# A transformer block with routed experts: parts of an expert's list and register loads become steps of the attention's plan

## The chip, the cores and the metric

The kernel runs on one core of a Trainium2 chip. The metric is the device time of one execution in microseconds (us), as the median of several. Engines are named as in the profile: PE multiplies matrices (PEld is its weight load, which overlaps), DVE is the vector engine, ACT the scalar engine, POOL GpSimd, SP SyncE, which only issues DMAs here. Each engine works through its own queue in order.

## The reference, cut to what matters

```python
# B = 2 batches of T = 2048 tokens, D = 256; 2 heads of 128 with one shared K and V; 8 experts, FF = 1024
mod = (silu(c) @ wmod).reshape(B, 6, 1, D)          # sa, ca, ga, sb, cb, gb
h = layernorm(x) * (1 + ca) + sa
k = rope(h @ Wk.T); v = h @ Wv.T; q = rope(einsum('btd,hkd->bhtk', h, Wq))
w = softmax(where(causal, q k^T / sqrt(128), -inf))
x = x + ga * ((w v) @ Wo.T)

h = layernorm(x) * (1 + cb) + sb
gate = softmax(h @ Wg + bg)                          # [4096, 8]
thr = sigmoid(h @ Wt + bt) / 8
w = relu(gate - thr);  w = w / sum(w)                # many entries are zero
u = gelu(einsum('td,edf->etf', h, W1) + b1)
x = x + gb * einsum('te,etd->td', w, einsum('etf,efd->etd', u, W2) + b2)
```

All is float32. A token has to be worked on only by the experts for which its weight is not zero; the kernel makes use of that.

## The kernel before

The program has two phases.

**Attention.** `attention()` handles 32 tiles of 128 tokens (16 of each batch), in groups that alternate between the batches: `(0,4),(1,4)` three times, then `(0,2),(1,2),(0,1),(1,1),(0,1),(1,1)`. It doesn't emit instructions directly. Every piece of work is a step that is given to a plan: `plan.add(engine, cost, do, after, take, give, rank, late)`. `cost` is a written estimate of its time, `late` what passes until its effect is there (a DMA's landing), `take` and `give` count buffers, and a low `rank` goes first. `Plan.run` (L36 to L88) simulates the engines with these costs, takes for a free engine the ready step with the lowest rank, and emits all steps in the order so found. On the chip this order is fixed for each engine.

For a tile the steps are: layer norm, transposition, projections, scores (L528 on PE, then a copy with maximum L539 on DVE and the exponential L555 on ACT), transposed probabilities (L601, L605), the sums with V (pav, L611), projection (L645), residual (L652), second layer norm (L412 to L419, L667, L670), writing of the normalised features to a table in HBM (`feats`), and the gate's logits (L692 and on). For each group, `gate_steps` works out each token's weight for each expert, and the place that it takes in that expert's list (`place`, `entry`). One list for each expert lies in HBM; an entry holds the token's number and weights. List 0 is written during attention: one indirect DMA of POOL for each tile (`scatter`, L808), each after the one before.

Three further things are done in attention, with rank 1000, so behind everything else: the front of list 0 is read (`read_front`, L906), and expert 0's first 512 entries that lie in it are worked on ahead, as two items of 256 tokens (AHEAD = 2). An item is: `fetch` (gather of the tokens' features by POOL, L884; transposition by a DMA of SP, L893; `join` on DVE, L899), `first` (W1, PE, L950), `act` (Gelu, ACT, L958), `second` (W2, PE, L967), `result` (DVE, L974 to L979). Then the whole sheet of list 0 is read (L1005), `behind` (DVE, L1012) takes the numbers of the item that follows, and `fetch` brings its columns to `kept.xT`. `total` (PE and DVE, L852 to L871) sums up how many tokens each expert has, and how many items; the counts lie in `counts`.

**Experts.** `experts()` has a loop for each engine, over experts and items, with semaphores between the engines and with the counts in registers. `count` loads a count into an engine's register (L1038, a TENSOR_LOAD on that engine's queue), at the head of each engine's part or at each expert. An item of expert e takes 256 tokens of its list (the last one may be half as wide):

- POOL copies the numbers from the sheet (L1299) and gathers the features (L1257); SP transposes them (L1103); DVE joins them into xT (L1199).
- PE: h = W1 (L1145), y = W2 (L1136), ACT: Gelu between them (L1171).
- DVE scales with weight and modulation (L1208, L1214, L1223, L1235), POOL adds the rows to the output by an indirect DMA (L1288).

While expert e runs, POOL writes list e+1 with `write`: NP = 8 parts of NW = 4 tiles, one part (four scatters, L1278) for each item of expert e, and in front of the first item those parts for which e has no items. SP reads the sheet of e+1 (L1093) after as many turns of its loop as there are parts in items (`a`), once all parts are written. ACT issues the weight load for expert e+2 when it begins expert e (L1180, L1183).

Part 0 of list 1 is written once before the loop (`write(1, 0, 0)`), so that the semaphore `written` starts one part up, and once more in the loop.

Of the kernel before, what the change touches and what calls it, by code (L numbers as in the profile page):

```python
# [18 lines left out]
ALU = mybir.AluOpType  # L19
AX = mybir.AxisListType  # L20

P = 128
# [10 lines left out]
NW = 4  # L33
NP = NTOK // P // NW
AHEAD = 2
AHEAD_TILES = 24  # L36
SC = 512
# [64 lines left out]
def adaln_block_kernel(ctx, tc, x, wqkvT, woT, wgt, bgt, w1, b1T, w2, b2, cT, wmod, rope, out):  # L102
# [50 lines left out]
        who=const.tile([P, CI], I32, name="who"),  # L153
        xT=const.tile([P, KD, TI], F32, name="xT"),
    )

# [36 lines left out]
def attention(  # L193
# [83 lines left out]
    l_c = load(c_sb, cT.rearrange("(k p) b -> p k b", p=P), 2)  # L277
    l_x0 = None
    wm = wmod.rearrange("(k p) f -> p k f", p=P)
# [144 lines left out]
    def tile_steps(b, i, r, group, g):  # L424
# [225 lines left out]
        def resid():  # L650
            for h in range(NH):
# [3 lines left out]
                )  # L655

        n_a = add("ACT", 0.38, aT_out, n_p[-1:], take=["aT"], give=["pav"])
        n_o = add("PE", 0.87, proj, [n_a, m_wo[b]], take=["ps"], give=["aT"])
# [57 lines left out]
    def gate_steps(b, i0, m, q, group, after):  # L716
# [89 lines left out]

        def scatter(j):
            nc.gpsimd.indirect_dma_start(  # L808
                out=lists[0],
                out_offset=bass.IndirectOffsetOnAxis(ap=place[:, at + j, 0:1], axis=0),  # L810
                in_=entry[:, at + j, 0, :],
                in_offset=None,
            )
# [7 lines left out]
        n = add("DVE", 1.2, places, [n_c, n_w], give=["ps"])  # L821

        for j in range(m):
            listed.append(plan.add(
                "POOL", 1.1, lambda j=j: scatter(j), after=[n] + listed[-1:], rank=r + 10.0,
                late=1.5,
            ))
        return n

    order_w, listed, last_exp = [], [], []  # L830
    groups = [(0, 4), (1, 4)] * 3 + [(0, 2), (1, 2), (0, 1), (1, 1), (0, 1), (1, 1)]
    begun, q = [0] * B, 0
    for b, m in groups:
        group, ends = {}, []
        for j in range(m):
            ends.append(tile_steps(b, begun[b] + j, float(q + j), group, j))
        last = gate_steps(b, begun[b], m, q, group, ends)
        begun[b] += m
        q += m
        if q == AHEAD_TILES:  # L840
            listed_ahead = list(listed)

            def filled(group=group):
                pf = ps_tile("pf")
                nc.tensor.matmul(pf[:, :1], ones, group["sum"][:, :1], start=True, stop=True)
                nc.vector.tensor_scalar(flag, pf[:, :1], float(AHEAD * TI), None, ALU.is_ge)

            n_flag = plan.add("PE", 0.2, filled, after=[last], take=["ps"], give=["ps"], rank=q)

    def total():  # L850
# [14 lines left out]
        )  # L865
        nc.vector.reduce_sum(n, more, axis=AX.X)
        nc.vector.tensor_copy(counts[:, E : 2 * E], n)
        nc.vector.tensor_scalar(
            counts[:, 2 * E : 3 * E], n, -1.0, float(NP), ALU.mult, ALU.add
        )  # L870
# [5 lines left out]

    def fetch(index, u, after, to, take=()):

# [28 lines left out]

    n_front = low("SP", 0.1, read_front, listed_ahead + last_score, late=2.5)

# [12 lines left out]
    for k in range(AHEAD):  # L922
# [61 lines left out]
        for f0 in range(0, NF, 2):  # L984
            n = low(
                "PE", 1.74, lambda f0=f0, first=first: first(f0), [n_x, l_first[0]] + before_gelu,
                take=["ps"], give=["s"] if f0 == NF - 2 else [],
            )
            n_a.append(low(
                "ACT", 1.0, lambda f0=f0, act=act: act(f0), [n, l_b1] + before_gelu + n_a[-1:],  # L990
                take=["s"], give=["ps"],
            ))
        n = None
        for c in range(CI):
            for f0 in (0, NF // 2):
# [5 lines left out]
                )  # L1001
        low("DVE", 1.5, result, [n, n_g, l_b2], give=["ps", "size"])

    n_s = low(
        "SP", 0.1, lambda: nc.sync.dma_start(kept.sheet, sheet_of_0), listed, late=2.0  # L1005
    )
# [11 lines left out]

    n = low("DVE", 0.4, behind, [n_s, n_flag])
    fetch(lambda c: next_at[:, c : c + 1], "_next", [n], lambda: kept.xT)  # L1020

    plan.add("PE", 0.2, total, after=[last, n_flag], take=["ps"], give=["ps"], rank=q)
    plan.run()
    ctx.close()


def experts(
# [6 lines left out]
    LAG = 2  # L1034
    xT, who, yo = kept.xT, kept.who, kept.yo[-1]

    def count(eng, at, most):
        return nc.values_load(  # L1038
            counts[0:1, at : at + 1], engines=[eng.engine],
            skip_runtime_bounds_check_because="from a sum of 0s and 1s over all tokens",  # L1040
            min_val=0, max_val=most,
        )

# [34 lines left out]
    with tc.tile_critical():  # L1078
# [7 lines left out]
        with nc.Block() as block:  # L1086

            @block.sync
            def _(sync):
                def read(e):  # L1090

                    sync.wait_ge(sem["written"], (e * NP + 1) * (16 * NW))
                    sync.dma_start(  # L1093
                        sheets[e], lists[e].rearrange("(p c) f -> p c f", p=P)
                    ).then_inc(sem["read"], 16)
# [11 lines left out]
                for e in range(E):  # L1107
                    many = items_of(sync, count(sync, e, NTOK))
                    if e == E - 1:
                        run(sync, many, NTOK // TI, lambda i: turn(t0 + i))  # L1110
                    else:
                        a = count(sync, E + e, NP)
                        run(sync, a, NP, lambda i: turn(t0 + done + i))
# [13 lines left out]
            def _(pe):  # L1127
# [31 lines left out]
                pe.sem_inc(sem["taken"], 1)  # L1159
                n = [count(pe, e, NTOK) for e in range(E)]  # L1160
                items(pe, n, item, begin)

            @block.scalar
            def _(act):
# [22 lines left out]
                act.sem_inc(sem["second"], 4)  # L1187
                items(act, [count(act, e, NTOK) for e in range(E)], item, begin)

            @block.vector  # L1190
            def _(dve):
# [50 lines left out]

                n = [count(dve, e, NTOK) for e in range(E)]
                skip = count(dve, 3 * E, AHEAD * CI)
                dve.sem_inc(sem["ready"], 2)
# [3 lines left out]
            def _(pool):  # L1249
# [13 lines left out]

                def write(e, c, w=None):

                    if w is None:
                        w = c + (e - 1) * NP
                        wait("written", w * (16 * NW) + 16 * NW)
                        w = w + 1
                    pool.tensor_copy(  # L1270
# [59 lines left out]
                pool.sem_inc(sem["biased"], AHEAD)  # L1330
                write(1, 0, 0)
                skip = count(pool, 3 * E, AHEAD * CI)
                done, t0 = 1, 0
                for e in range(E):
                    many = items_of(pool, count(pool, e, NTOK))
                    if e > 0:
# [3 lines left out]
                    else:  # L1340
                        a, front = count(pool, E + e, NP), count(pool, 2 * E + e, NP)

                        def part(c):
                            write(e + 1, nc.s_assert_within(c, 0, NP - 1,
                                skip_runtime_bounds_check_because="a part of a list"))

                        run(pool, front, NP, part)
                        run(pool, a, NP, lambda i: item(
# [19 lines left out]
                single = pool.snap(  # L1368
                    ((count(pool, E - 1, NTOK) + (P - 1)) >> 7) & 1, min_val=0, max_val=1
                )  # L1370
# [54 lines left out]
```

## Time and profile before

| | |
|---|---|
| median of 3 runs | 1676.8 us (1675.76 to 1677.0) |
| profiled execution | 1677.0 us, span of its instructions 1675.2 us |
| granted TensorE clock, mean | 0.988 |
| PE busy | 1622.3 us, 97% |
| POOL busy | 855.0 us, 51% |
| DVE busy | 677.0 us, 40% |
| ACT busy | 576.4 us, 34% |
| last matmul of the items ahead ends | 499.5 us |
| first matmul of the experts' loops | 506.9 us |

"Busy" is the time in which an engine runs instructions; loads of registers, branches, semaphores and the issue of DMAs don't count as busy. In a line of the table of groups, `L1145 PE MATMUL h<-xT,w ... x2752 | 660.6, 373 | 16.3 <-DVE xT L1199 8.9` means: line 1145 of the kernel, on PE, matmuls that write h from xT and w, 2752 of them, 660.6 us busy, 373 ns on average, and before them PE stood idle for 16.3 us, of which 8.9 us ended with the release by DVE's line 1199. In a line of a timeline the start comes first, then the length, and in brackets the idle time of the engine before it and what ended it. A `q` behind an engine's name is its sequencer (DMA issue, register loads). "PEclk" is the granted clock as a share of full speed.

### The profile page before, as it was taken

How to read it: one execution, taken by the hardware profiler on the slowest of the kernel's cores; microseconds unless marked ns; L12 is line 12 of the kernel's file. 1: busy time of each engine (PE TensorE's matmuls, PEld its weight loads, DVE VectorE, ACT ScalarE, POOL GpSimd, SP SyncE). 2: the span in 40 equal slices, each digit the busy share in tenths (PEclk: the TensorE clock that was granted, in tenths of full speed). 3: DMA queues.
4: the chain of work that ended last, by engine and by line, in shares of the span. 5: the costliest groups of instructions: out<-in, count | busy, mean ns of one | idle time of the engine just before them, and what ended most of it. 6: DMA issues, size and time to landing. Idle time of an engine off the chain costs nothing.

```text
span 1675.2 us, 26699 instructions
## 1 busy us (share of the span) xinstructions
PE 1622.3 (97%) x7666; PEld 1352.3 (81%) x7666; DVE 677.0 (40%) x2220; ACT 576.4 (34%) x1390; POOL 855.0 (51%) x991
## 2 busy tenths in 40 slices
PE   6999999999998998999999999999999999999996
PEld 3667677676787887888888888888888888888886
DVE  5987767666642222322333222222322222222322
ACT  2555555555632222222222222222222232222222
POOL 2332222021117777756775775676677477734443
PEclk9999999999998998999999999999999999999998
DMA  6211000000024334335334433533533333433332
GB/s 218 101 39 32 26 29 29 17 13 17 13 50 101 57 63 109 58 58 108 58 60 101 78 57 61 106 59 62 109 60 61 63 58 57 67 59 57 63 57 47
DMA packets 166045, 106.36 MB, mean 63 GB/s; under 512 B 111136, under 2 KB 157344, under 8 KB 165856
## 3 DMA queue, kind: packets, MB, share of 16 engines
q0 software_dynamic: 42064, 46.84, 17.8%
q1 hardware_dynamic: 116048, 46.22, 11.7%
q10 hardware_dynamic: 7872, 12.58, 2.4%
q8 instruction: 26, 0.43, 0.1%
q14 instruction: 35, 0.29, 0.1%
HBM read 50.39 MB, written 31.87 MB: 49 GB/s over the span
## 4 chain that ended last, share of the span: by engine, by line
PE 61%; DMA 3%; issue 3%; POOL 3%; POOLq 1%; DVE 0%; SPq 0%; DVEq 0%
PE h L1145 31%; PE y L1136 30%; POOL out L1288 2%; DMA xp<-xr 1%; DMA xr<-feats,at 1%; POOL list L1278 0%; POOL xr L1257 0%; DMA out<-yo,who 0%; POOLq L1038 0%; POOL out L1320 0%; POOL at L1299 0%; POOLq L1086 0%; POOLq L1299 0%; DVE yo L1235 0%; POOL to L1270 0%
## 5 line engine op out<-in xcount | busy, mean ns | idle before, releaser
L1145 PE MATMUL h<-xT,w 128*128 128x256 f32 (+1 forms) x2752 | 660.6, 373 | 16.3 <-DVE xT L1199 8.9
L1136 PE MATMUL y<-w,g 128*128 128x256 f32 x2640 | 654.3, 379 | 0.0
L1171 ACT ACTIVATE g<-h,b_sb 128x256 f32<-128x256 f32 (+1 forms) x688 | 320.4, 466 | 847.8 <-PE h L1145 845.7
L1145 PEld LDWEIGHTS h<-xT,w 128*128 128x128 f32 x2752 | 514.7, 191 | 86.6 <-DVE xT L1199 10.5
L1136 PEld LDWEIGHTS y<-w,g 128*128 128x128 f32 x2640 | 498.8, 190 | 66.3
L1288 POOL DMA_INDIRECT out<-yo,who x173 | 283.2, 1637 | 215.1 <-DVE yo L1235 163.0
L1199 DVE COPY xT<-xp 128x512 uint16<-128x512 uint16 x172 | 68.0, 437 | 630.4 <-PE h L1145 608.0
L1278 POOL DMA_INDIRECT list<-new,to x228 | 233.7, 1025 | 99.3 <-POOL new L1273 46.7
L1257 POOL DMA_INDIRECT xr<-feats,at x172 | 173.8, 1010 | 100.9 <-POOL at L1299 70.2
L611 PE MATMUL pav<-pT,v 128*128 128x256 f32 x544 | 144.0, 387 | 0.6 <-ACT pT L605 0.5
L528 PE MATMUL psc<-kT,qT 128*128 128x512 f32 (+3 forms) x320 | 142.9, 532 | 0.3 <-DVE s L539 0.2
L539 DVE TENSOR_SCALAR_CACHE_REDUCE s<-psc 128x512 f32<-128x512 f32 (+3 forms) x160 | 96.2, 605 | 68.3 <-PE psc L528 46.0
L555 ACT ACTIVATE s<-s,nmx 128x512 f32<-128x512 f32 (+3 forms) x160 | 103.9, 651 | 46.5 <-DVE nmx L546 46.2
L611 PEld LDWEIGHTS pav<-pT,v 128*128 128x128 f32 x544 | 96.1, 192 | 29.1 <-issue 19.6
L1223 DVE TENSOR_TENSOR yb<-y,b_bc 128x256 f32<-128x256 f32 x165 | 62.6, 419 | 135.9 <-PE y L1136 135.8
L418 POOL TENSOR_SCALAR rstdf<-mvf 128x1 f32<-128x1 f32 x32 | 8.3, 260 | 195.2 <-DVE mvf L414 115.4
L605 ACT COPY pT<-ptr 128x512 f32<-128x512 f32 (+1 forms) x144 | 77.2, 563 | 52.3 <-PE pav L611 30.4
L601 PE MATMUL ptr<-ident,s 128*128 128x128 f32 x544 | 76.4, 280 | 2.7 <-ACT s L555 2.7
L601 PEld LDWEIGHTS ptr<-ident,s 128*128 128x128 f32 x544 | 65.6, 145 | 16.6 <-ACT s L555 5.0
L1214 DVE SCALAR_TENSOR_TENSOR gate<-gb_bc,mcur,part 128x256 f32<-128x256 f32 x172 | 75.8, 482 | 3.0
L808 POOL DMA_INDIRECT list<-entry,place x32 | 33.7, 1054 | 76.9 <-DVE place L805 56.6
L528 PEld LDWEIGHTS psc<-kT,qT 128*128 128x128 f32 x320 | 57.5, 190 | 14.0 <-issue 6.3
(157 smaller groups left out, 1069.7 us busy)
## 6 DMA issues: line engine op xcount, KB each, us to landing
w<-in_w ACTq DMA_DIRECT2D x12, 1024.0 KB, 7.8
x<-in_x SPq DMA_DIRECT2D x32, 128.0 KB, 2.1
out<-x SPq DMA_DIRECT2D x32, 128.0 KB, 1.7
w<-in_w SPq DMA_DIRECT2D x4, 1024.0 KB, 9.1
feats<-hp SPq DMA_DIRECT2D x32, 128.0 KB, 1.7
list<-new,to POOLq DMA_INDIRECT x228
out<-yo,who POOLq DMA_INDIRECT x173
xr<-feats,at POOLq DMA_INDIRECT x172, 2.8
```

The costliest lines, as they stand in the source:

```text
L528: nc.tensor.matmul(ps[:, :w], st["qT"][:, h, :], kT[:, ds(c * SC, w)], start=True, stop=not last)
L539: nc.vector.tensor_scalar(s[:, :w], st["sc", h, c][:, :w], 1.0, None, ALU.mult, ALU.max, accum_out=st["mx", h][:, c : c + 1],)
L555: nc.scalar.activation(s[:, :w], s[:, :w], AF.Exp, bias=st["nmx", h], accum_out=st["den"][:, h, c : c + 1],)
L601: nc.tensor.transpose(ptr[:, j, h, :], s[:, ds((c0 + j) * P % SC, P)], ident)
L605: nc.scalar.copy(pT[:, :m], st["ptr", c0][:, :m])
L611: nc.tensor.matmul(st["pav"][:, : NH * P], v[:, c0 + j, :], st["pT", c0][:, j].rearrange("p h t -> p (h t)"), start=(c0 + j == 0), stop=(c ...
L1136: last = pe.matmul(ys[c], gs[f % 4][:, ts(c, P)], weights[e][1][:, f, :], start=(f == 0), stop=(f == NF - 1),)
L1145: last = pe.matmul(hs[f % 4][:, :w], weights[e][0][:, k, ts(f, P)], xT[:, k, :w], start=(k == 0), stop=(k == KD - 1),)
L1171: act.activation(gs[f % 4][:, :w], hs[f % 4][:, :w], AF.Gelu_apprx_tanh, bias=b1_sb[:, at : at + 1],).then_inc(sem["act"], 1)
L1257: pool.indirect_dma_start(out=xr[:, ts(c, 2 * D)], out_offset=None, in_=feats, in_offset=bass.IndirectOffsetOnAxis(ap=at[:, c : c + 1], ax ...
L1278: pool.indirect_dma_start(out=lists[e], out_offset=bass.IndirectOffsetOnAxis(ap=to[:, j : j + 1], axis=0), in_=new[:, j, :], in_offset=Non ...
L1288: pool.indirect_dma_start(out=rows, out_offset=bass.IndirectOffsetOnAxis(ap=who[:, c : c + 1], axis=0), in_=yo[:, c, :], in_offset=None, b ...
```

## The change

1. A constant FRONT = 2. The first two parts of list 1 (8 tiles of batch 0) are written by steps of the plan, as those of list 0 are. In the loops, list 1 has six parts left, and the count of parts for expert 0 is at most six. `written` starts at 16, by one scatter that writes the first tile's entries again, and the waits for it are rewritten to match.
2. The loads of the counts into registers become steps of the plan (`hold`), one for each engine, of rank 1000: PE's after `total` and the last matmul ahead, ACT's after the last Gelu ahead, DVE's after `behind`, POOL's after `total`, SP's after the read of the sheet. Counts that aren't held are loaded in the loops as before.
3. `behind` and the next item's `fetch` have rank 999 instead of 1000.
4. `read_front` waits only for the scatters of list 0 that it reads, and no longer for the last tile's scores too. The matmuls of the items ahead wait for the last tile's last sum with V (`last_sum`) instead of the last exponential.
5. `total` is a step with `late=2.0`, and limits the parts for expert 0 (two small DVE operations more).

```diff
+FRONT = 2
+        last_sum[:] = n_p[-1:]
@@ gate_steps
-        def scatter(j):
+        def scatter(e, j):
             nc.gpsimd.indirect_dma_start(
-                out=lists[0],
-                out_offset=bass.IndirectOffsetOnAxis(ap=place[:, at + j, 0:1], axis=0),
-                in_=entry[:, at + j, 0, :],
+                out=lists[e],
+                out_offset=bass.IndirectOffsetOnAxis(ap=place[:, at + j, e : e + 1], axis=0),
+                in_=entry[:, at + j, e, :],
                 in_offset=None,
             )
...
         for j in range(m):
-            listed.append(plan.add(
-                "POOL", 1.1, lambda j=j: scatter(j), after=[n] + listed[-1:], rank=r + 10.0,
-                late=1.5,
-            ))
+            for e in (0, 1):
+                if e == 0 or at + j < FRONT * NW:
+                    listed[e].append(plan.add(
+                        "POOL", 1.1, lambda e=e, j=j: scatter(e, j), after=[n] + listed[e][-1:],
+                        rank=r + 10.0 * (e + 1), late=1.5,
+                    ))
@@ total
         nc.vector.reduce_sum(n, more, axis=AX.X)
+        nc.vector.tensor_scalar(n[:, :1], n[:, :1], float(NP - FRONT), None, ALU.min)
@@ items ahead
-    n_front = low("SP", 0.1, read_front, listed_ahead + last_score, late=2.5)
+    n_front = low("SP", 0.1, read_front, listed_ahead, late=2.5)
...
-                "PE", 1.74, lambda f0=f0, first=first: first(f0), [n_x, l_first[0]] + before_gelu,
+                "PE", 1.74, lambda f0=f0, first=first: first(f0),
+                [n_x, l_first[0]] + last_sum,
...
-    n = low("DVE", 0.4, behind, [n_s, n_flag])
-    fetch(lambda c: next_at[:, c : c + 1], "_next", [n], lambda: kept.xT)
-    plan.add("PE", 0.2, total, after=[last, n_flag], take=["ps"], give=["ps"], rank=q)
+    n_behind = next_("DVE", 0.4, behind, [n_s, n_flag])
+    fetch(lambda c: next_at[:, c : c + 1], "_next", [n_behind], lambda: kept.xT, low=next_)
+    n_total = plan.add(
+        "PE", 0.2, total, after=[last, n_flag], take=["ps"], give=["ps"], rank=q, late=2.0
+    )
+    def hold(name, eng, columns):
+        def load():
+            kept.count[name] = {at: register(nc, eng, counts, at) for at in columns}
+        return load
+    skip = 3 * E
+    low("PE", 2.0, hold("PE", nc.tensor, range(E)), [n_total] + n_ahead)
+    low("ACT", 2.0, hold("ACT", nc.scalar, range(E)), [n_total] + n_a)
+    low("DVE", 2.2, hold("DVE", nc.vector, [*range(E), skip]), [n_total, n_behind])
+    low("POOL", 1.0, hold("POOL", nc.gpsimd, [skip, 0, E, 2 * E]), [n_total])
+    low("SP", 0.5, hold("SP", nc.sync, [0, E]), [n_total, n_s])
@@ experts, SP
-                    sync.wait_ge(sem["written"], (e * NP + 1) * (16 * NW))
+                    sync.wait_ge(sem["written"], (e * NP - FRONT) * (16 * NW) + 16)
@@ experts, all engines
-        return nc.values_load(...)
+        held = kept.count[eng_name[eng.engine]]
+        return held[at] if at in held else register(nc, eng, counts, at)
@@ experts, POOL
-                def write(e, c, w=None):
-                    if w is None:
-                        w = c + (e - 1) * NP
-                        wait("written", w * (16 * NW) + 16 * NW)
-                        w = w + 1
+                def write(e, d):
+                    first = FRONT if e == 1 else 0
+                    w = d + ((e - 1) * NP - FRONT if e > 1 else 0)
+                    c = nc.s_assert_within(d + first, first, NP - 1, ...)
+                    wait("written", w * (16 * NW) + 16)
...
-                write(1, 0, 0)
+                pool.indirect_dma_start(
+                    out=lists[1],
+                    out_offset=bass.IndirectOffsetOnAxis(ap=place[:, 0, 1:2], axis=0),
+                    in_=entry[:, 0, 1, :],
+                    in_offset=None,
+                ).then_inc(sem["written"], 16)
```

## The prediction

> **What bounds the kernel now.** I read the page first, for the engine that is busy, then its table of costly groups, for the idle time in front of that engine's groups, and then windows and timelines around that idle time.
>
> ```profile
> PE 1622.3 (97%) x7666; PEld 1352.3 (81%) x7666; DVE 677.0 (40%) x2220; ACT 576.4 (34%) x1390; POOL 855.0 (51%) x991
> L1145 PE MATMUL h<-xT,w 128*128 128x256 f32 (+1 forms) x2752 | 660.6, 373 | 16.3 <-DVE xT L1199 8.9
> ```
>
> PE is the bound, at 97%. The change adds and removes no matmul, so it can only act on PE's idle time (1675.2 - 1622.3 = 52.9 us of the span) and on what idle time costs afterwards through the clock. In the second phase the whole idle time in front of the first matmul of an item is 16.3 us, and nearly all of it lies in two places. The windows cut there show both:
>
> ```profile
> core 0: us, PE busy (x) PEld busy (x) DVE busy (x) ACT busy (x) POOL busy (x), PEclk, DMA share, GB/s
> 462.00:500.00 38.00, 37.46 (x184) 32.45 (x183) 15.99 (x76) 14.74 (x30) 7.67 (x9) 1.00 0.21 51
> 500.00:507.00 7.00, 0.14 (x1) 0.15 (x1) 1.69 (x5) 0.00 (x0) 3.36 (x4) 0.63 0.24 29
> 507.00:523.30 16.30, 16.30 (x64) 13.93 (x65) 2.47 (x7) 3.79 (x8) 11.39 (x16) 0.84 0.57 167
> 523.30:627.20 103.90, 103.90 (x497) 91.56 (x496) 31.98 (x86) 29.50 (x64) 76.27 (x86) 1.00 0.36 60
> 627.20:636.20 9.00, 0.06 (x2) 0.04 (x1) 0.85 (x3) 0.00 (x0) 6.08 (x6) 0.74 1.00 286
> 636.20:652.70 16.50, 16.50 (x64) 14.08 (x65) 3.45 (x11) 3.79 (x8) 12.22 (x15) 0.83 0.33 55
> 652.70:1662.00 1009.30, 1009.30 (x4769) 890.26 (x4768) 298.34 (x835) 283.35 (x608) 627.66 (x651) 1.00 0.39 68
> ```
>
> The first place is the step from attention to the experts' loops (500 to 507), the second is expert 0's last item (627.2 to 636.2). From 652.7 to 1662 PE has no gap at all. The clock column matters: the item after each gap runs at 0.83 to 0.84, and its 64 matmul rows take 16.3 and 16.5 us, where an item at clock 1.00 takes 13.85 (103.90 us for seven and a half). So a gap costs its own length and about 2.7 us more.
>
> Why the second gap is there, from the timeline:
>
> ```profile
> 617.56 0.35 SPq L1093 DMA_DIRECT2D sheet<-list  x1
> 625.97 0.38 ACTq L1180 DMA_DIRECT2D w<-in_w  x1
> 626.54 1.58 SPq L1103 DMA_TRANSPOSE xp<-xr  x1
> 635.35 0.76 DVE L1199 COPY xT<-xp 128x512 uint16<-128x512 uint16 x2 [9.83 <-DMA xp<-xr]
> 636.17 1.22 PE L1145 MATMUL h<-xT,w 128*128 128x256 f32 x2 [8.94 <-DVE xT L1199]
> ```
>
> SyncE reads expert 1's sheet after eight turns, because list 1 is written in eight parts, one for each item of expert 0, which has nine items here. The gather for expert 1's first item then starts at 621.84, its transposition is issued at 626.54, behind the 1 MB weight load of 625.97, and ends 8.5 us after it. DMA share is 1.00 in that window. Usually this transposition takes 3.1 us.
>
> Why the first gap is there, from the waits and the register loads of the counts:
>
> ```profile
> PEld h L1145 <- DVEq L1038: 7.8, 1, 7.8
> PE h L1145 <- DVEq L1038: 7.4, 1, 7.4
> L1038 DVEq TENSOR_LOAD <-counts x9: 299/310/570, 503.1 to 506.3; - x9
> L1038 PEldq TENSOR_LOAD <-counts x8: 294/306/622, 502.8 to 505.5; - x8
> ```
>
> The last matmul of the items ahead ends at 499.46. DVE copies xT until 501.73, all engines meet, and then DVE loads nine counts (503.1 to 506.6) before it says that xT is ready; PE's first matmul follows at 506.86.
>
> **The change, part by part.**
>
> *Two parts of list 1 are written during attention.* L1278 falls from 228 to 217: 36 scatters for list 1 before (a part was written twice), now 6 x 4 and one that only moves the count. The sheet of expert 1 is now due after six parts: two turns earlier, two items of 13.8 = 27 us. Its gather can then go when xr is free, in place of behind the sheet. The trace holds this very case: at expert 1 to 2, where the sheet is long there, the gather is issued 6.3 us before the half item, the transposition at 775.76, before the weight load at 783.11, and PE goes on at 784.20 with no gap. Two turns of slack are many times what is needed. So the 8.94 us go, and the clock stays: 8.94 + 2.7 = **-11.7 us**. What is late next is nothing on PE: ScalarE's weight load follows the transposition, as at 783.
>
> *Eight more scatters in the plan (L808, 32 to 40).* Eight times 1.074 us (the median of L808) on POOL, which is about a quarter busy in attention. Each waits for the one before in the same list, 2.2 us to landing, where the plan writes 1.1 + 1.5; queued behind such a wait on POOL stand the small moments of the next tile (L418, L419), on which DVE's normalisation waits. L808 already waited for itself 14 times for 17.5 us, with no PE gap to show for it: PE's gaps from 71 to 455 add up to only some 4 us. Bounds: 0 (all beside PE) and 8 x 1.07 = 8.6 us x a tenth reaching PE. I take +0.3. Here a rule speaks against the change. L808 takes 1.074 us in attention, with DVE two thirds busy, and L1278 0.977 in the experts' loops, with DVE a third busy: 0.1 us apiece, 0.8 us in all, under POOL's idle time. The Trainium skill, "SBUF — State Buffer", section "A bandwidth-pool intuition that's wrong (but worth ruling out)", says that VectorE can lock GpSimd out of the shared port, and that a DMA whose descriptors GpSimd writes then took some 3100 ns in place of 620. By that factor of five, eight scatters would cost 8 x 1.07 x 4 = 34 us of POOL; with a tenth of it on PE the sum below would be -10. The trace has 32 of these scatters among the same work, the longest at 1.271; I go by it.
>
> *Front of the sheet of list 0 read earlier.* The read (SP), the gathers (POOL, 2 x 1.2), the weights and gates (DVE, seven operations, 2.6 us in all by their rows) and the joins move from the last tile of the batch pair two tiles up, since the read no longer waits for the last scores. SP queues it in front of a tile's `out`, and DVE's part may wait for the landing, with scores' maxima behind it that ScalarE's exponentials wait for. The plan counts 2.5 us of landing and the trace has 1.5; but the scatters it waits for land 0.7 us a link later than planned. I put DVE's wait at 1.8 us, of which half reaches PE: +0.9. In return, the 2.12 us gap at 454.95 (ScalarE's exponentials late, beside the present read at 452.63) may shrink, and its cold time of 1.7 us too; of the 3.8 I take a tenth off: -0.4. DVE's two more tiny operations in the counting step: +0.15. Attention together: 0.3 + 0.9 - 0.4 + 0.15 = **+1.0 us**, bounds -2 (most of the gap of 455 gone) and +4 (a new gap like it, with its cold clock).
>
> *The matmuls of the items ahead wait for the last tile's last sum, not its exponential.* In the order of the instructions PE's queue near its end stays all but the same: the first of them follows the last pav, as before. I cost this at 0; what hides it is PE itself, which is full there (37.46 of 38.00).
>
> *The counts as steps of the plan, the next item's columns in front.* DVE's nine loads now stand between next_at and the first result, where DVE is 42% busy (15.99 of 38): 3.5 us off the path, at 0. ACT's eight stand behind its last Gelu, POOL's and SP's early: 0. PE's eight, though, stand at the very end of PE's queue, behind its last matmul: 499.46 + 3.0 (their time in the trace) = 502.5, where DVE is ready at 501.73. Everyone then meets 0.8 us later than now. From there, before: DVE came out 1.37 us after its xT, and PE started 0.26 us after DVE's last load. So PE starts at 502.5 + 1.37 + 0.26 = 504.1; PE's own entry to its loop, at most 1.06 us after its last load, gives the same. 506.86 - 504.1 = **-2.7 us**. Bounds: -1 (loads are slower while DMA runs: single ones took 622 ns) and -3.5. PE idles some 4.6 us still. Does the clock go cold? In this trace the gap of 2.12 us at 455 was followed by a clock of 0.5 from 457.5, that of 7.40 went cold 2.2 us in, that of 8.94 only 4.3 us in. The Trainium skill, "TensorE: Matmul & The Clock Gate", "What's actually happening", has half clock after about one idle window of 3.4 us that runs free of the program. By the rule 4.6 us is a matter of luck and the sum may be -16.0 (2.6 us more); by the rows it is -13.4, as two of three gaps were cold sooner. I leave the cold item in.
>
> Weights of expert 2 are now issued some 2 us earlier (505.14 before), and the first gather's transposition comes later than the landing of 7.8 us: 0.
>
> **Sum**, against the profiled execution (span 1675.2, time 1677.0, so 1.8 us lie around the span; it is 0.2 above the median of 1676.8): -11.7 - 2.7 + 1.0 = -13.4. Span 1661.8; from the median, **1663.4 us**.
>
> **The rivals.**
>
> A, *the second gap does not close entirely*. The transposition may still fall beside the weight load, take 8.5 us for 3.1, and PE be short and cold. For: that load and the transposition are 0.57 us apart now. Against: expert 1 to 2. Left of the gain: some 6 us; 1669.5.
>
> B, *the register loads give nothing*: PE's eight at its tail and the meeting take what DVE's gave. For: PE had to pass them in both kernels. Against: DVE's 9 ended last. 1663.4 + 2.7 = 1666.
>
> C, *slower*: two of the sixteen score buffers are taken by the items ahead's columns, now from two tiles earlier on. The last tiles want eight for each pair of scores, and tile 14's scores move a chunk later. If the scores then come late for ScalarE, each of the last four or five tiles gets a gap like that of 455 (2.12 + 1.7 cold = 3.8): 15 to 19 us, some 1681 with the rest gained. It decides from four and a half such gaps on (17 us). Against: the queue orders from tile 15 on are the same, and PE has half a microsecond idle in 462 to 500.
>
> D, *nothing*: expert 0 might not have been the late one; 1676.8. Against: the timeline above.
>
> **How the numbers follow.** Forecast 0.73, A 0.09, B 0.11, C 0.05, D 0.02. The range runs from 1658.5 (gap of 455 gone, or the clock kept at the first gap) to 1670.0 (A; or +4 in attention and -1 at the loads: 1668): the bounds of the unknown costs. About 0.2%, 3.4 us, is what a measurement of this kernel can tell from no change. Faster by more takes the forecast, A, B: 0.93; same D and an edge of C and A: 0.03; slower C: 0.04.
>
> **What would show it.** Right: no gap before the first h of expert 1 and no clock of 0.5 there; L1278 x217 and L808 x40; a gap of about 4.6 us before the first item, named for something other than DVE's loads, clock cold after it; the sheet of expert 1 read two items sooner. Wrong: gaps of PE before the last tile's sums that add up to 8 us and more above today's 6 (C); an xT of expert 1 that still waits for its transposition (A); a start of the experts' loops, measured from the last matmul ahead, still over 7 us (B).

## The result and the profile after

The changed kernel takes 1669.7 us, median of 6 runs (1668.3 to 1670.7), beside 1676.9 for the kernel before: ratio 0.9954, 95% interval 0.9941 to 0.9967. The forecast was 1663.4, with a range of 1658.5 to 1670.0: the sign was right and the time lies at the range's upper end, so about 6 us of the forecast gain are missing. The profiled execution took 1670.7 us, with a span of 1668.9, 6.3 under that of before.

The page of the changed kernel, busy time and the group of the first matmuls of an item:

```profile
PE 1622.3 (97%) x7666; PEld 1352.3 (81%) x7666; DVE 677.7 (41%) x2222; ACT 576.4 (35%) x1390; POOL 854.2 (51%) x982
L1186 PE MATMUL h<-xT,w 128*128 128x256 f32 (+1 forms) x2752 | 657.6, 372 | 4.4 <-DVEq L1286 4.4
```

PE's busy time is the same to a tenth, but two changes cancel in it: from the first item of the loops on it is 3.3 us shorter (one item less at half clock), and in attention 3.3 us longer. In front of the items PE's idle time fell from 16.3 us to 4.4, in one place. Windows of the changed kernel, cut at the last matmul ahead (508.2) and the first item (512.5):

```profile
core 0: us, PE busy (x) PEld busy (x) DVE busy (x) ACT busy (x) POOL busy (x), PEclk, DMA share, GB/s
460.00:508.20 48.20, 46.04 (x227) 39.58 (x225) 19.09 (x88) 20.53 (x45) 7.49 (x10) 0.96 0.09 24
508.20:512.50 4.30, 0.00 (x0) 0.00 (x0) 2.26 (x7) 0.00 (x0) 0.12 (x1) 0.76 0.01 4
512.50:528.00 15.50, 15.49 (x61) 13.30 (x62) 2.36 (x7) 3.79 (x8) 10.66 (x12) 0.85 0.65 187
528.00:640.00 112.00, 112.00 (x536) 98.94 (x535) 35.01 (x97) 31.86 (x69) 79.93 (x87) 1.00 0.43 80
640.00:1655.00 1015.00, 1015.00 (x4795) 895.28 (x4795) 300.48 (x836) 284.61 (x611) 635.74 (x659) 1.00 0.39 69
```

The second gap is gone (528 to 1655 without an idle moment), the first is 4.35 us long, and the item after it runs at 0.85. But the last matmul ahead ends at 508.16, where it ended at 499.46: **attention has become 8.7 us longer**. The timeline of the changed kernel at the step from expert 0 to 1:

```profile
596.67 0.35 SPq L1134 DMA_DIRECT2D sheet<-list  x1
...
631.37 0.38 ACTq L1221 DMA_DIRECT2D w<-in_w  x1
631.46 0.77 DVE L1240 COPY xT<-xp 128x512 uint16<-128x512 uint16 x2 [2.35 <-PE h L1186]
...
632.46 2.77 PE L1186 MATMUL h<-xT,w 128*128 128x256 f32 x12
```

The sheet is read 35.8 us before expert 1's first matmul (18.6 before the change; counted from the first matmul of the loops, 26.5 us sooner, where the prediction has 27). DVE's copy waits for PE, not for the transposition. The waits and loads at the start of the loops, in the changed kernel:

```profile
PE h L1186 <- DVEq L1286: 4.4, 1, 4.4
L1060 DVEq TENSOR_LOAD <-counts x9: 301/309/554, 498.8 to 502.1; - x9
L1060 PEldq TENSOR_LOAD <-counts x8: 300/308/772, 504.1 to 507.6; - x8
```

Where attention lost time shows in the groups of PE between 60 and 500 us: idle time ahead of the transposed probabilities and of the transposed second norm. First the kernel before:

```profile
L601 PE MATMUL ptr<-ident,s 128*128 128x128 f32 x524 | 73.4, 280 | 2.7 <-ACT s L555 2.7
L692 PE MATMUL ph<-ident,hx 128*128 128x128 f32 x62 | 12.5, 286 | 2.1 <-DVE s L539 1.4 <-DVE hx L670 0.3 <-ACT pT L605 0.3
```

and the same groups in the changed kernel:

```profile
L602 PE MATMUL ptr<-ident,s 128*128 128x128 f32 x528 | 73.1, 280 | 5.1 <-ACT s L556 3.2 <-DVE col L800 1.7 <-DVE s L540 0.2
L694 PE MATMUL ph<-ident,hx 128*128 128x128 f32 x62 | 12.4, 286 | 5.0 <-DVE hx L672 2.3 <-DVE s L540 2.0 <-ACT pT L606 0.4
```

All gaps of PE of 0.15 us or more from 60 us to the last matmul ahead add up to 7.6 us before and 13.4 after. New ones end at 192.6 (2.09), 243.7 (0.98), 277.6 (1.72) and 347.7 (0.58). The clock was at half for 3.4 us twice in that stretch before and three times after, which costs 1.7 us each time. The 5.8 us of gaps and 1.7 for the cold stretch make 7.5. Another 1.6 had passed at 29 us, where the queues are still alike and the first full clock came at 22.3 us instead of 17.1; over all fourteen profiles that moment lies between 15.1 and 23.8, so this part is chance. The three make 9.1, 0.4 more than the 8.7: gaps under 0.15 us shrank by 0.2, and 0.2 are not itemised.

### The profile page after: what moved, and what is told of

Its sections match the earlier page's. It is cut to its first block, busy times and chain, and to the rows that moved or that the text cites. A ratio compares the mean times of both kernels' runs of the same rounds, so it can differ in the third digit from the quotient of the medians.

```text
span 1668.9 us, 26686 instructions
## 1 busy us (share of the span) xinstructions
PE 1622.3 (97%) x7666; PEld 1352.3 (81%) x7666; DVE 677.7 (41%) x2222; ACT 576.4 (35%) x1390; POOL 854.2 (51%) x982
## 4 chain that ended last, share of the span: by engine, by line
PE 68%; issue 0%; DMA 0%; POOLq 0%; DVE 0%; DVEq 0%; POOL 0%
PE h L1186 34%; PE y L1177 34%; DMA out<-yo,who 0%; POOLq L1127 0%; DVE yo L1276 0%; POOL out L1332 0%; DVE yb L1264 0%; DVEq L1474 0%; DVEq L1127 0%; DVE who L1268 0%; POOLq L1424 0%; POOLq L1332 0%; DVEq L1273 0%; POOLq L1426 0%; POOLq L1292 0%
## 5 line engine op out<-in xcount | busy, mean ns | idle before, releaser
L1322 POOL DMA_INDIRECT list<-new,to x216 | 222.7, 1031 | 93.6 <-POOL new L1317 44.2
L810 POOL DMA_INDIRECT list<-entry,place x40 | 42.1, 1052 | 106.9 <-DVE place L807 87.0
L1343 POOL COPY at<-sheet 128x2 int32 x85 | 63.1, 742 | 12.9 <-DMA xp<-xr 12.9
```

What stands on the lines that cost most here:

```text
L1322: pool.indirect_dma_start(out=lists[e], out_offset=bass.IndirectOffsetOnAxis(ap=to[:, j : j + 1], axis=0), in_=new[:, j, :], in_offset=Non ...
```

## Experiments

Three theories for the longer attention are told apart: (1) the eight scatters hold POOL back; (2) as steps they change the order that the plan finds; (3) the earlier read of the front costs. Time is the median of the run's kernel in us, ratio that to the kernel before on the same chip. "Ahead ends" and the gaps are from each profile: end of the last matmul ahead, PE's gaps from 60 us to there, gap before the first item.

| run | time | ratio (95%) | ahead ends | gaps | first gap |
|---|---|---|---|---|---|
| before | 1676.9 | | 499.5 | 7.6 | 7.40 |
| after | 1669.7 | 0.9954 (0.9941-0.9967) | 508.2 | 13.4 | 4.35 |
| e1_spread | 1670.2 | 0.9959 (0.9945-0.9972) | 507.0 | 12.5 | 4.41 |
| e2_unplanned | 1663.2 | 0.9922 (0.9908-0.9935) | 499.9 | 7.5 | 4.38 |
| e3_front_old | 1671.0 | 0.9963 (0.9949-0.9977) | 508.4 | 13.9 | 4.38 |
| e5_unpl_front_old | 1660.5 | 0.9906 (0.9893-0.9920) | 497.9 | 7.6 | 4.38 |
| e4_no_front | 1674.5 | 0.9993 (0.9986-0.9999) | 499.8 | 7.6 | 4.40 |
| e6_before_replanned | 1682.6 | 1.0040 (1.0026-1.0054) | 502.8 | 10.1 | 7.34 |
| e7_loads_in_loops | 1665.6 | 0.9937 (0.9923-0.9951) | 500.0 | 7.6 | 7.34 |
| e8_filled | 1661.3 | 0.9911 (0.9897-0.9924) | 497.3 | 5.8 | 6.72 |
| e9_columns_first | 1685.7 | 0.9899 (0.9872-0.9925) | 496.9 | 6.0 | 5.18 |
| e10_landing | 1682.8 | 0.9884 (0.9854-0.9914) | 501.1 | 9.8 | 4.40 |
| e11_loads_last | 1681.3 | 0.9915 (0.9892-0.9938) | 495.4 | 6.0 | 3.72 |
| e12_landing_again | 1679.1 | 0.9916 (0.9891-0.9942) | 499.9 | 8.2 | 4.38 |

The kernel before took 1677.7 us beside the first four experiments, 1675.8 beside the next four, and 1703.6 and 1694.0 beside the last two pairs. There a wait appears in the loops, at the half-wide items, that the other profiles lack. The kernel before has no profile from these chips, so its share of that wait isn't known, and these four ratios carry it on both sides; the part up to the first item is the safer comparison.

### Do the eight scatters hold POOL back?

At the new gap of 192.6 it looks so. Timeline of the changed kernel:

```profile
188.62 1.08 POOL L810 DMA_INDIRECT list<-entry,place  x1 [0.19 <-issue]
189.05 0.18 DVE L415 BATCH_NORM_AGGREGATE mvf<-stf 128x2 f32<-128x6 f32 x1
190.00 0.97 POOL L810 DMA_INDIRECT list<-entry,place  x1 [0.30 <-issue]
191.00 0.24 POOL L419 TENSOR_SCALAR rstdf<-mvf 128x1 f32<-128x1 f32 x1
...
192.09 0.48 DVE L672 SCALAR_TENSOR_TENSOR hx<-hx,rstdf,mod_bc 128x256 f32<-128x256 f32 x1 [0.46 <-POOL rstdf L420]
...
192.63 0.33 PE L694 MATMUL ph<-ident,hx 128*128 128x128 f32 x1 [2.09 <-DVE hx L672]
```

The tile's moments (mvf) are there at 189.2, but their scale (rstdf) waits on POOL behind two scatters until 191.0, and PE waits for the normalised tile (hx). The first experiment keeps the plan and moves only the emission of list 1's scatters (`owed` is a list):

```diff
+                    do = lambda e=e, j=j: scatter(e, j)
+                    if e == 1:
+                        do = lambda do=do: owed.append(do)
...
                 st["hp"], st["hx"].bitcast(U16).rearrange("p (d two) -> p two d", two=2)
             )
+            if i >= 8 and owed:
+                owed.pop(0)()
```

> The order of PE, DVE, ACT and SP is that of the changed kernel to the last instruction. Only POOL's eight scatters of list 1 are issued elsewhere: one behind each copy of the halves of tiles 8 and up (L679), not in bursts behind the scatters of list 0. Theory 1 (the burst of scatters on POOL holds back the small moments L419 and L420 behind it, and so hx and PE: the 2.09 us gap at 190.5 and the cold clock of 1.7 us that follows): 1669.7 - 3.8 = 1666, and the gap at 190 is gone. Theory 2 (the eight steps make the plan come out in another order for PE and DVE, and the order itself has the gaps): 1669.7, all gaps as before. Theory 3 (the front of the sheet, read earlier, is what costs): 1669.7.

1670.2 us: nothing gained. In the traces PE, DVE and ACT have the same order of instructions in this run as in the changed kernel. The timeline shows why the gap stays:

```profile
187.82 0.18 DVE L416 BATCH_NORM_AGGREGATE mvf<-stf 128x2 f32<-128x6 f32 x1
188.10 0.22 POOL L420 TENSOR_SCALAR rstdf<-mvf 128x1 f32<-128x1 f32 x1 [1.26 <-DVE mvf L416]
...
189.39 0.62 DVE L498 TENSOR_TENSOR t<-pq,rope_sb 128x192 f32<-128x192 f32 x2
189.92 0.47 DVE L670 SCALAR_TENSOR_TENSOR hx<-x,mvf,mod_bc 128x256 f32<-128x256 f32 x1
...
191.04 0.44 PE L697 MATMUL ph<-ident,hx 128*128 128x128 f32 x2 [1.73 <-DVE hx L673]
```

POOL is now done with rstdf's first part at 188.3, and the gap is still 1.73: DVE's queue has rotations and score maxima ahead of hx, and PE's queue asks for hx at that place. The wait is in the order of the two queues; POOL stood in front of 0.36 us of it. Theory 1 falls.

### Or the order that the plan finds?

In the second experiment the scatters are no steps of the plan at all. They are issued at the same later places:

```diff
+            def both(j=j):
+                scatter(0, j)
+                if at + j < FRONT * NW:
+                    owed.append(lambda: scatter(1, j))
+            listed[0].append(plan.add(
+                "POOL", 1.1, both, after=[n] + listed[0][-1:], rank=r + 10.0, late=1.5,
+            ))
```

> The eight scatters are no steps of the plan at all; they are issued behind the halves of tiles 8 and up, as in the run with the spread scatters. The plan then orders PE and DVE as in the kernel before up to tile 13, where the earlier read of the front still moves a few steps. Theory 1 (POOL's burst): as with the spread scatters, 1666. Theory 2 (the order that the eight steps bring about): the gaps between 100 and 350, 5.8 us, and the cold clock of 1.7 go: 1662.2. Theory 3 (front read): 1669.7.

1663.2 us, 6.9 less than the first experiment beside it, with the same scatters issued in the same way, behind the halves of later tiles; only the order of the rest differs. In its trace PE has the order of the kernel before up to 361 us. PE's groups between 60 and 500 us, of this run, are those of before again:

```profile
L603 PE MATMUL ptr<-ident,s 128*128 128x128 f32 x524 | 72.4, 278 | 2.8 <-ACT s L557 2.7
L697 PE MATMUL ph<-ident,hx 128*128 128x128 f32 x62 | 12.3, 282 | 2.1 <-DVE s L541 1.4 <-DVE nmx L548 0.3 <-ACT pT L607 0.3
```

Next a kernel in which nothing is added or removed, the kernel before with one number that only the plan reads:

```diff
-                late=1.5,
+                late=1.2,
```

> The kernel before, with one number changed that only the plan reads: the landing written for a scatter of list 0 is 1.2 us instead of 1.5. No instruction is added or taken away, but some 180 of PE's 1815 rows stand elsewhere. If the order found for the kernel before is a good one among many, and any change in the plan's times exchanges it for another (theory 2 in its general form), attention gets several us longer: +2 to +8, 1680 to 1685. If only the eight steps themselves do harm: 1677 as before.

1682.6 us, 0.40% slower than before. Gaps in attention rose from 7.6 to 10.1 us, and the last matmul ahead ended 3.3 us later. That profiled execution was the quickest of its runs (1680.6), so the profile shows less than the medians do; the rest of the 6.8 us isn't itemised.

The same number changed in the changed kernel, where the eight scatters are steps as the change made them:

> The changed kernel with the landing of the plan's scatters written as 1.2 us instead of 1.5, a number that only the plan reads (the trace has 2.2 from issue to landing, of which the plan counts 1.1 as cost). No instruction differs, but 181 of PE's 1815 rows stand elsewhere. If the length of attention is a draw from many orders (theory 2 in its general form), it changes by some us in either direction: outside 1669.7 +- 1.5. If the eight steps do the harm wherever they come to stand: 1669.7.

> The changed kernel with the landing written as 1.2 us, once more, as its first run was on a chip on which every kernel took longer. There its last matmul ahead ended at 501.1, 7.1 us sooner than in the changed kernel. If that holds, it takes 1669.7 - 7 = 1663 where the kernel before takes 1677, as fast as the run with unplanned scatters: the eight scatters themselves cost nothing that can be seen, whatever way they are issued. If the shorter attention was that one execution's: 1669.7.

Two runs on two chips: ratios of 0.9884 and 0.9916, and the last matmul ahead at 501.1 and 499.9 instead of 508.2. Counted from PE's first gap over 0.4 us behind 60 us (71 to 73 us), so without the chance of the start-up, attention is 5.6 and 7.5 us shorter. PE's groups of the second one:

```profile
L602 PE MATMUL ptr<-ident,s 128*128 128x128 f32 x524 | 71.7, 278 | 3.6 <-ACT s L556 3.2 <-DVE hT L464 0.2
L694 PE MATMUL ph<-ident,hx 128*128 128x128 f32 x62 | 12.5, 286 | 1.6 <-DVE hx L672 0.9 <-DVE s L540 0.6
```

So eight scatters issued in bursts as planned steps cost nothing that shows, under a luckier order; the same edit of one number cost the old kernel 6.8 us and saved the new one 5.6 and 7.5 us of attention. Theory 2 holds in its general form: added steps shift the plan's clock, and the plan comes out with another order whose length on the chip it doesn't foresee.

### Does the earlier read of the front cost?

```diff
-    n_front = low("SP", 0.1, read_front, listed_ahead, late=2.5)
+    n_front = low("SP", 0.1, read_front, listed_ahead + last_score, late=2.5)
```

> The changed kernel, but the read of the front of list 0's sheet waits for the last tile's scores again, as in the kernel before. Theories 1 and 2: 1669.7, the gaps between 100 and 350 stay. Theory 3 (the earlier read costs; DVE waits 3.5 us for its landing): 1669.7 - 3.5 = 1666 or less. The prediction put this part at +0.5.

> Both: the scatters of list 1 outside the plan and spread over later tiles, and the front read at its old place. PE's queue in attention is then that of the kernel before. If nothing in attention costs but the order (theory 2): 1677 - 11.7 - 3.1 = 1662; the difference to the run with unplanned scatters alone is the price of the earlier front read (theory 3: 3.5 us, the prediction: 0.5). Theory 1: 1666 if scatters hold POOL back wherever they stand, else 1662.

On the change itself: 1671.0, no gain; theory 3 doesn't explain the loss. In the trace of the changed kernel DVE does wait 3.5 us for the front, until 359.5, but PE has no gap beside it. On the run with unplanned scatters: 1660.5 against 1663.2, with overlapping intervals. In the trace of 1660.5 (e5) PE's whole order up to the loops is that of the kernel before. In that of 1663.2 (e2) DVE has score maxima in that place and doesn't wait for the front, and the gaps are equal (7.6 and 7.5). Their two profiled executions, 3.5 us apart in span, have one and three cold stretches of 3.4 us from 60 us to the last expert's end. Whether 2 us between them are a cost of the earlier read or of how the gaps fell stays open.

### The two terms that the forecast rested on

```diff
-FRONT = 2
+FRONT = 0
```

> The changed kernel with FRONT = 0: list 1 is written wholly in the loops, in eight parts, and its sheet is read after eight turns as in the kernel before; register loads, ranks and the front's read as in the change. The prediction's step: expert 1's first item waits again for its transposition, 8.9 us and 2.7 us of cold clock. Theory 2 (the plan's new order costs 7.5 us and comes from the eight steps alone) says that attention is as short as in the run with unplanned scatters, so 1663.2 + 11.7 = 1675. Rival (the order is not to blame): 1669.7 + 11.7 = 1681. If the wait goes away by the ranks or by the register loads alone, 1663.

1674.5 us. The waits of that run at expert 1:

```profile
DVE xT L1240 <- DMA xp<-xr: 9.8, 1, 9.8
...
PE h L1186 <- DVE xT L1240: 8.9, 1, 8.9
```

The gap is back, 8.87 us, and the cold item after it. Against the run with unplanned scatters the ratios differ by 0.9993 - 0.9922 = 0.0071, 11.9 us of 1677, by their intervals to within some 2.5: the forecast's term was 11.7.

```diff
-        held = kept.count[eng_name[eng.engine]]
+        held = {}
...
-    low("PE", 2.0, hold("PE", nc.tensor, range(E)), [n_total] + n_ahead)
...
```

> The run with unplanned scatters, but all counts are loaded at the loops again, none in the plan. The prediction's step says that the gap before the first item grows by 3 us, from 4.4 to 7.4, ended by DVE's loads: 1663.2 + 3.0 = 1666.2. Rival B (the loads gave nothing): 1663.2, the gap stays at 4.4.

1665.6 us, a ratio 0.0015 above that of the run with the loads in the plan, 2.5 us of 1677; the intervals overlap, so the gap decides. Its wait line:

```profile
PE h L1187 <- DVEq L1061: 7.3, 1, 7.3
```

The gap is 7.34 us again, by DVE's loads: 2.96 more, forecast 3.0. Rival B falls.

### A better version

The gap of some 2 us that every order tried so far kept near the last tile (457 before, 465.8 after) can take one `first` step of the items ahead:

```diff
-                [n_x, l_first[0]] + last_sum,
+                [n_x, l_first[0]] + (last_score if k == 0 and f0 < FILL else last_sum),
```

with FILL = 2, and the last `result` after the last `join`.

> The run with unplanned scatters, and two things more: the first matmuls of the items ahead (one step of 1.7 us) may go after the last tile's last scores, where PE waits 2.1 us for the exponentials (at 457), and the next item's columns are joined by DVE ahead of the last result. If PE's gaps are what counts: -1.7 at 457 and up to -1.7 for the clock that stays warm there, -0.75 before the first item: 1659 to 1661. If the score buffers and PSUM banks that the early matmuls hold delay the last tile: no gain, 1663 or more.

1661.3 us, a ratio of 0.9911 against 0.9922 for the run it starts from, with overlapping intervals. The gap was filled and PE's last matmul ahead came at 497.3, but the first item started at 504.0, hardly sooner than 504.3: most was given back to a new wait. Timeline of DVE in that run:

```profile
491.77 0.15 DVE L1031 TENSOR_TENSOR next_at<-sheet 128x2 int32<-128x2 int32 x1
491.96 0.22 DVE L1034 SCALAR_TENSOR_TENSOR next_at<-next_at,flag,sheet 128x2 int32<-128x2 int32 x1
499.61 0.76 DVE L914 COPY xT<-sign_p_next 128x512 uint16<-128x512 uint16 x2 [7.43 <-DMA sign_p_next<-g_sb_r_next]
```

Two steps follow this chain back: the gates and first result behind next_at, then POOL's loads behind the gather.

```diff
+            n_g = low("DVE", 1.7, gates, [n_w, n_behind] + m_wo, take=["size"])
...
-            "DVE", 1.5, result, after + [n_next] * (k == AHEAD - 1), give=["ps", "size"]
+            "DVE", 1.5, result, after + [n_g, n_next if k == AHEAD - 1 else n_behind],
+            give=["ps", "size"],
```

> The filled kernel, with DVE's last steps in another order: the next item's numbers (next_at) ahead of the first result and of the gates of the second item ahead. In the filled kernel's trace the sheet has landed by 488.3, next_at runs only at 491.77, the gather and transposition follow, and the last join waits for them until 499.6, 2.3 us after PE's last matmul. If that wait is what ate the gain of the filled gap: next_at some 3 us sooner, first item 2.5 to 3 us sooner, gap before it 3.7 to 4.4 in place of 6.7: 1661.3 - 2.7 = 1658.6. If another step ends last there (the first result, which DVE now takes later, with the second item's PSUM behind it): 1661.

```diff
-    low("POOL", 1.0, hold("POOL", nc.gpsimd, [skip, 0, E, 2 * E]), [n_total])
+    low("POOL", 1.0, hold("POOL", nc.gpsimd, [skip, 0, E, 2 * E]), [n_total, n_next])
```

> The kernel with the columns first, and POOL's four loads of counts behind the next item's gather. In that kernel's trace next_at is done at 488.4 and the gather starts only at 490.6, with the loads between them; the last join then waits for its transposition until 497.76, 0.8 us after PE's last matmul. If the loads are what held it: gather 2 us sooner, the join done ahead of PE's last matmul, the first item's gap 3.7 to 4.3 in place of 5.2, and the time 1 us under that of the columns first: some 1659 where the kernel before takes 1677. If the first result and its barrier end last anyway: no change, gap 5.2.

The first did in part what was expected: the first item starts at 502.1 after a gap of 5.2 us, where 3.7 to 4.4 were expected (504.0 and 6.7 in the filled kernel). next_at came 3.7 us sooner, at 488.0, but POOL's loads then held the gather until 490.6. The second took that away: gather at 487.1, first item at 499.1, gap 3.7:

```profile
PE h L1202 <- DVEq L1302: 3.7, 1, 3.7
```

The whole times, 0.9899 and 0.9915 of before, came from the chips with the extra waits in the loops, of which one shows in the waits of the first of them, from 615 to 622 us:

```profile
PE y L1193 <- ACT g L1228: 2.7, 3, 1.7
```

Their intervals overlap that of the filled kernel, so the last 5 us to the first item are shown by the profile but not by the total. Any of e2, e5, e8, e9 and e11 beats both kernels; which of them is best isn't settled.

## Why the prediction was right, and where a term was mis-sized

- *What bounds the kernel*: right. PE stayed the bound at 97%, and only its gaps and the clock behind them moved.
- *Second gap, -11.7*: right. It closed wholly: from their first matmul to PE's last, the loops take 1143.5 us in place of 1155.7, 12.2 less; 11.9 by the ratios of the runs with and without the two parts. Rival A, a transposition still beside the weight load, didn't occur: the transposition was ready well ahead, as at expert 1 to 2.
- *Register loads, -2.7*: right in size (-3.05 in the gap), by some luck: two steps were wrong and partly cancel. PE's eight loads were put at 3.0 us behind its last matmul. They ran from 504.1 to 507.9, while the array still worked until 508.16, so they added nothing. What ends last is DVE's last result and join of xT (508.19 to 510.4), 2.26 us behind the last matmul where 3.0 were forecast; then the meeting of all engines, 2.1 where 1.63 were. POOL's four loads, costed at nothing, did stand ahead of the next gather: it starts 1.1 us behind next_at in the changed kernel, where this is hidden, and 2.2 in e9, where it shows.
- *Clock after the first gap*: the choice of the row over the rule was right; the item ran at 0.85, and the clock went cold in all eight profiles with a first gap of 4.35 to 4.41 us. (The gap of 7.40 went cold 2.4 us in, not 2.2.)
- *Attention, +1.0 with bounds of -2 and +4*: this is the term that failed; it was +8.7. Of that, some 7.1 came with the order (gaps, and a cold stretch behind one of them) and 1.6 with the start-up's chance. The step at fault is "Eight more scatters in the plan": it priced the scatters as work on POOL (+0.3) and looked for their neighbours in POOL's queue. Their own cost was right, about nothing. But of PE's 2274 matmuls ahead of the loops only 1844 keep their order in the trace, by the names of their tiles, the first change being at 107.7 us; the order found for the kernel before was taken as given. That PE's queue stays all but the same near its end was true, and beside the point: the gaps lie at 192, 244, 278 and 348 us. The front's terms of +0.9 and -0.4 did not come either: DVE waited 3.5 us where 1.8 were forecast, but nothing of it reached PE, and the gap of 2.12 us stayed as it was.
- *The rule on the shared port*: the trace decided rightly. L810 took 1.052 us on average with 40 of them, 1.054 with 32 before.
- *Rival C* had the sign, a loss in attention, but not its place: after 348 us the one gap of 2.12 us is left that the kernel before has too.

Gains of 12.2 and 3.05 against losses of 8.7 in attention and 0.3 behind the last matmul leave 6.3, as the spans differ. That the time still lies in the range, by 0.3 us, is luck: +8.7 in attention is over twice the bound of +4, and the range's end came from rival A and from a sum in which attention cost no more than 4.

## What to carry to other kernels

Where a list scheduler with written costs fixes the order, an added step has two prices: its work, and a new draw of the order. The second can be several times the first, in either direction; compare the order of all queues before and after, and where it changed widely, widen the range by what a change of one cost does to it. To add side work to a tuned plan, issue it outside the plan behind an instruction that is there already, or try a few values of a number that only the plan reads and keep the best.

A gap that is filled shows who was second: here the next item's sheet, gather and transposition, each held by small steps in front of it on DVE and POOL.

## What the runs showed of the hardware that was not expected

All changes of the clock in these traces lie whole multiples of 3.413 us apart. The window of that length is as the Trainium skill has it ("TensorE: Matmul & The Clock Gate", section "What's actually happening"), but a window needn't be idle throughout. I cut all fourteen traces into such windows from 60 us on and took PE's idle share in each. At full clock, all 32 windows with 60% idle or more were followed by half clock, and none below 28% was. Of the 65 between, 13 were; what decides there stays open (the same stretch near 120 us, at 32%, went cold in the kernel before and in e4, and not in e2, e5 and e8). At half clock, the 24 windows with 21% idle or more were followed by another one at half clock, the 45 with 7% or less were not.

So a gap of 2.12 us goes cold when it falls within one window (62% at 454.1 in the kernel before) and doesn't when it is split (28 and 34% in e5_unpl_front_old). That is 1.7 us for each such gap, by chance, in each execution. A gap of 4.1 us leaves no such chance: even shared evenly, 2.05 us are 60% of each window. This fits the first gap of some 4.4 us, which always went cold: by these windows it was no matter of luck, as the prediction read the rule.
